# Row sums through HBM in the last image, position terms by transfer, and one addition fewer in cv1

## The chip, the cores and the metric

The kernel runs on one core of a Trainium2 chip. The metric is the device time of one execution in microseconds, and the time of a kernel is the median of several runs. The kernel before takes 2314.39 us (median of 7 runs, 2313.59 to 2315.1). Its profiled execution took 2314.33 us, and the span that the profile covers is 2312.8 us of these, so 1.5 us lie outside it.

All arithmetic is float32. "An image" below is one of the eight elements of the batch, counted 0 to 7. Engines: PE multiplies matrices, DVE and ACT work on vectors, POOL and SP mostly issue transfers.

## The reference

```python
def bot_attention(x, qkv_w, rw, rh):                    # x: 256 channels, 32 x 32 positions
    qkv = conv2d(x, qkv_w, 0).reshape(b, 3, HEADS, HD, hw)   # 4 heads of 64 channels, hw = 1024
    q, k, v = (qkv[:, 0], qkv[:, 1], qkv[:, 2])
    r = (rw + rh).reshape(1, HEADS, HD, hw)             # position terms, one per channel and position
    logits = jnp.einsum('bhdi,bhdj->bhij', q, k + r) * HD ** (-0.5)
    a = jax.nn.softmax(logits, axis=-1)
    return jnp.einsum('bhij,bhdj->bhdi', a, v).reshape(b, c, h, w)

def _L0_conv_ref(x, ...):                               # x is group-normed, 512 channels
    t = cbs(x, cv1_w, cv1_bn, 0)                        # cbs: convolution, batch norm, silu
    ys = [t[:, :C], t[:, C:]]
    for i in range(N):                                  # N = 2 bottlenecks
        yi = ys[-1]
        z = cbs(yi, m_cv1_w[i], m_cv1_bn[i], 1)         # 3x3
        z = bot_attention(z, m_qkv_w[i], m_rw[i], m_rh[i])
        z = jax.nn.silu(bn_eval(conv2d(z, m_cv2_w[i], 0), m_cv2_bn[i]))
        ys.append(yi + z)
    return cbs(jnp.concatenate(ys, axis=1), cv2_w, cv2_bn, 0)

x = x + _L0_conv_ref(_gn(x), ...)                       # eight images
```

## The kernel before

**Stages.** The loop at L1325 runs over the eight images. Each image goes twice (n = 0 and n = 1) through a 3x3 convolution by Winograd tiles (`conv3x3`, L955, matmuls on L970), a projection to q, k and v (`project_strassen`, L611), the attention (`attention_fast`, L709) and a 1x1 convolution (`m2`, L988). Image 0 projects in its n = 0 stage with the plain `project`. The 1x1 convolution cv1 of the next image is done inside the n = 0 stage of the image before; for images 1 to 6 it is one level of Strassen, seven products in place of eight (`strassen_cv1`, L1123). cv2 follows the n = 1 stage.

**Attention.** Queries and heads form four groups (L717): groups 0 and 1 are the two halves of the queries for the first head pair, groups 2 and 3 the same for the second. A group takes its 1024 keys in four pairs of 128-key blocks (L720). For each pair PE makes logits into two PSUM tiles (L734), ACT takes the exponential into an SBUF tile `pt` (L738, three such tiles), DVE adds it to the running sum `acc` of the group (`add_up`, L747), and PE multiplies `pt` by v into the PSUM tile `av_ps` (`times_v`, L757). PE runs one pair ahead: the logits of pair i stand before the product of pair i-1. When a group's product is complete, ACT copies one half of `av_ps` to `ao` (L775) and DVE adds the other (L776); only then may the next group's product overwrite `av_ps`, of which there is one.

**Row sums.** `acc` holds sums over the key blocks, and the 128 partitions are still to be added. After the first logits of the next group, `sums` (L778) does that with four small matmuls against ones (L786), a copy out of PSUM (L792) and a 4 KB store (L793). `spread` (L826), two pairs later, loads the sums (L823), takes the reciprocal `rc` (L830), stores it and loads it broadcast as `rs` (L834). `scale` (L842) multiplies `ao` by it in the next group but one. The last group is summed by `last_sums` (L796) with matmuls on L804, and `rs` is made from PSUM (L880, L881).

**Position terms.** `add_r` (L647) adds `rw` and `rh` to the keys with two DVE instructions a half. For the second head pair `later` (L703) does it, four DVE instructions of 128x512, after the first two pairs of the attention (L856).

**cv1.** `begin` runs at the end of the n = 0 attention: DVE makes eight sums `t_x` (L1159 to L1162), PE makes the products a11 b11 and s4 b22. `go_on` adds a12 b21 onto the first product in PSUM. After `m2`, `rest` makes s1 t1, s2 t2, s3 t3 and a22 t4, each copied out of PSUM by ACT (L1150). `add_y0` and `add_y1` combine them with six DVE additions of 128x1024 in groups 1 and 2 of the n = 1 attention.

**Order.** PSUM has three tiles of two banks under the name "big" for everything but `av_ps`; a new one waits until all readers of the tile in its place are done. Each engine runs its instructions in the order in which the build left them; `issue_after` puts an instruction behind another one of its engine, and the dictionary `behind` names the pair of the attention after which a function's instructions are put in. SP issues most transfers, POOL issues the output stores and residual loads; each issues in order.

Of the kernel before, what the change touches and what calls it, by code (L numbers as in the profile page):

```python
# [41 lines left out]
F32 = mybir.dt.float32  # L45
I32 = mybir.dt.int32
AF = mybir.ActivationFunctionType
ALU = mybir.AluOpType
# [4 lines left out]
P = 128  # L53
# [8 lines left out]
def kernel(  # L62
# [170 lines left out]
    def make_sq(n, tag, bufs):  # L233
        (a11, a12), (a21, a22) = ([block_qkv(n, o, i) for i in range(2)] for o in range(2))
        parts = [act.tile([P, 2, 3, P], F32, tag=tag, name="sq_new", bufs=bufs) for _ in range(2)]
        s1, s2, s3, s4 = (t[:, j] for t in parts for j in range(2))
        nc.vector.tensor_tensor(s1, a21, a22, ALU.add)
        nc.vector.tensor_tensor(s2, s1, a11, ALU.subtract)
        nc.vector.tensor_tensor(s3, a11, a21, ALU.subtract)
        nc.vector.tensor_tensor(s4, a12, s2, ALU.subtract)  # L240
        for h, t in enumerate(parts):
            nc.gpsimd.dma_start(sq_dram[n][:, 2 * h : 2 * h + 2], t)

    def load_sq(n):
        w = ring([P, 4, 3, P], "sq")
# [118 lines left out]
    def stages(act, small, ps_big, ps_av, n_pt):  # L364
# [246 lines left out]
        def project_strassen(n, z, sq, t):  # L611

# [88 lines left out]
                tt(q1, q1, u[:, 0], ALU.add)  # L701

            def later():  # L703
                for half in range(NH):
                    add_r(1, half)

            return q, kr, vT, later

        def attention_fast(n, z, at, behind, sq=None, t=None):  # L709

            q, kr, vT, later = (*project(n, z), None) if sq is None else project_strassen(n, z, sq, t)
            behind.get(-1, lambda: None)()

            ao = act.tile([P, NM, HW], F32, tag="z", name="ao")
# [6 lines left out]
            def logits(pair):  # L723
                g, j0 = pair[0]
                c, half = groups[g]
                pt = act.tile([P, PAIR, 2, HALF], F32, tag="pt", name="pt", bufs=n_pt)
                pts[pair[0]] = pt
                for i, (_, j) in enumerate(pair):
                    ps = ps_big.tile([P, 2, HALF], F32, tag="big", name="l_ps")
                    for hd in range(2):  # L730
                        r = slice(hd * HD, (hd + 1) * HD)
                        for kh in range(2):
                            o = j * P + kh * HD
                            nc.tensor.matmul(  # L734
                                ps[kh * HD : (kh + 1) * HD, hd, :], kr[r, c, o : o + HD],
                                q[r, c, ts(half, HALF)], start=True, stop=True,
                            )
                    exp = nc.scalar.activation(pt[:, i], ps, AF.Exp, scale=SCALE)  # L738
# [39 lines left out]
            def sums(g):  # L778
# [42 lines left out]
            def total(g, s_dram):  # L821

                nc.sync.dma_start(sums_all[:, at + g, :], s_dram.rearrange("a (i r) -> (a i) r", r=QP))  # L823
                return sums_all[:, at + g, :]

            def spread(g, s_dram):  # L826
# [3 lines left out]
                nc.vector.reciprocal(rc, total(g, s_dram))  # L830
# [12 lines left out]

            NQ = NJ // PAIR
            s_drams, rss, evicted = {}, {}, [None]
            for i in range(len(pairs) + 1):
                if i < len(pairs):  # L850
                    added = logits(pairs[i])
                    g, at_q = divmod(i, NQ)
                    with tc.issue_after(added.ins):
                        if at_q == NQ - 2 and g > 0:
                            rss[g - 1] = spread(g - 1, s_drams[g - 1])
                        if i == 1 and later is not None:  # L856
                            later()
                        if at_q == 1 and g > 1:
                            scale(g - 2, rss.pop(g - 2))
                if i > 0:  # L860
                    g, j0 = pairs[i - 1][0]
                    if j0 == 0 and g > 0:
                        s_drams[g - 1] = sums(g - 1)
                    times_v(pairs[i - 1])
                    if i < len(pairs) and accs.get(pairs[i][0][0], 0) is None:
                        with tc.issue_after(evicted[0].ins):
                            added = add_up(pairs[i])
                    with tc.issue_after(added.ins):
                        behind.get(g if j0 == 0 else (g, j0 // PAIR), lambda: None)()
# [253 lines left out]
        def strassen_cv1(w, sw, xts, y0, y1):  # L1123
# [31 lines left out]
            def begin():  # L1155
                t = [act.tile([P, 2, NM, HALF], F32, tag=tag, name="t_x") for tag in ("q", "k")]
                kept["t"] = t1, t2, t3, t4 = [t[i][:, j] for i in range(2) for j in range(2)]
                for c in range(2):
                    tt(t1[:, c], b12[c], b11[c], ALU.subtract)  # L1159
                    tt(t2[:, c], b22[c], t1[:, c], ALU.subtract)  # L1160
                    tt(t3[:, c], b22[c], b12[c], ALU.subtract)
                    tt(t4[:, c], t2[:, c], b21[c], ALU.subtract)  # L1162
                kept["ps"] = product(a11, b11)
                kept["m1"] = to(spare("xr", 2), kept["ps"])
                to(y0_2, product(s4, b22))

            def go_on():
                ps = product(a12, b21, kept["ps"])
# [1 line left out]
                    silu(y0[:, oc, ts(0, HALF)], ps[:, oc, :], bn_cv1 + oc)  # L1170

            def rest():
                t1, t2, t3, t4 = ([t[:, c] for c in range(2)] for t in kept["t"])
# [21 lines left out]
            return begin, go_on, rest, add_y0, add_y1, finish  # L1195

        def cv2_part(w2, ys, oc, ks=range(2 * NM)):

# [126 lines left out]
    for b in range(B):  # L1325
# [89 lines left out]
        ao, check = s.attention_fast(0, z, b * N * NM * NH, behind, sq.get(0), t)  # L1415
# [43 lines left out]

        def first():  # L1460
            if six:
                six[5]()
            if more:
                three[0]()
            else:
# [16 lines left out]
        ao, check = s.attention_fast(1, z, (b * N + 1) * NM * NH, behind, sq.get(1), t)  # L1482
# [105 lines left out]
```

## Time and profile before

| what | value |
|---|---|
| median of 7 runs | 2314.39 us (2313.59 to 2315.1) |
| profiled execution | 2314.33 us |
| its span | 2312.8 us |
| DVE busy | 1839.7 us (80%), 2920 instructions |
| ACT busy | 987.7 us (43%), 1292 instructions |
| POOL busy | 89.1 us (4%), 308 instructions |
| DMA moved | 235.60 MB, mean 102 GB/s |
| one image in the middle (622 to 905 us) | 283.00 us |

The table of engines gives the time that each was busy. PE counts two hardware matmuls for each float32 matmul of the kernel, so "x8" in a row of the trace is four matmuls of the source. The row "one image" is the repeat distance: four of the later images take the same 283 us to within the reading. The chain of waits follows the work that ended last back through the engines. A timeline gives each instruction or run of equal instructions with its start, its duration, and in brackets how long its engine was idle before it. A row for PEld is the loading of a matmul's weights.

### The profile page before, as it was taken

The page shows a single profiled execution, that of the slowest core. Times are in us where ns is not written, and L with a number is a line of the kernel's source. Part 1 is how long each engine was busy: PE and PEld are TensorE (multiplying, and loading weights), DVE is VectorE, ACT ScalarE, POOL GpSimd, SP SyncE. Part 2 cuts the span into 40 slices and gives each one's busy share as a digit, 9 for nine tenths or more (in the row PEclk, how much of TensorE's full clock was granted, in tenths as well). Part 3 has the DMA queues.
Part 4 walks back from the last instruction along what each step waited for, and adds up shares of the span by engine and source line. Part 5 has one row for each costly group of instructions (what it writes and reads, how often), then busy time and mean ns, then how long its engine had stood idle before and what let it go on. Part 6 is the DMA issues. An engine that isn't in the chain of part 4 may idle for free.

```text
span 2312.8 us, 36527 instructions
## 1 busy us (share of the span) xinstructions
PE 2287.2 (99%) x14806; PEld 1172.5 (51%) x14806; DVE 1839.7 (80%) x2920; ACT 987.7 (43%) x1292; POOL 89.1 (4%) x308
## 2 busy tenths in 40 slices
PE   7999999999999999999999999999999999999998
PEld 4546355463554636446364553646436364473633
DVE  8888878888788877887788887788877988777774
ACT  2443524435154452544525354253542535335352
POOL 1000000000000000000000000000000000000000
PEclk9999999999999999999999999999999999999999
DMA  7422334041430415213161221603116030260201
GB/s 239 174 86 87 120 127 161 16 151 34 168 124 21 140 44 201 82 50 111 52 238 38 77 87 47 250 29 102 60 47 250 29 133 29 76 221 16 87 11 62
DMA packets 95521, 235.60 MB, mean 102 GB/s; under 512 B 28016, under 2 KB 50736, under 8 KB 81904
## 3 DMA queue, kind: packets, MB, share of 16 engines
q1 hardware_dynamic: 83600, 182.84, 23.5%
q0 software_dynamic: 11744, 50.34, 5.7%
q8 instruction: 119, 1.95, 0.3%
q14 instruction: 58, 0.48, 0.1%
HBM read 198.54 MB, written 34.60 MB: 101 GB/s over the span
## 4 chain that ended last, share of the span: by engine, by line
PE 96%; DVE 3%; ACT 0%; DMA 0%; POOL 0%; issue 0%; SPq 0%; DVEq 0%; ACTq 0%
PE av_ps L768 19%; PE l_ps L734 19%; PE c_ps L970 14%; PE c L1028 8%; PE p_ps L630 8%; PE x_ps L1140 6%; PE c_new L1028 6%; PE m_ps L994 5%; PE ps L386 4%; PE pv_ps L634 3%; PE s_ps L786 1%; PE p_ps L634 1%; PE s_ps L804 1%; DVE acc L754 0%; PE v_ps L595 0%; DMA x<-in_x_dram 0%
## 5 line engine op out<-in xcount | busy, mean ns | idle before, releaser
L738 ACT ACTIVATE pt<-l_ps 128x1024 f32<-128x1024 f32 x512 | 494.9, 1023 | 410.0 <-PE l_ps L734 385.5
L754 DVE TENSOR_TENSOR acc<-acc,pt 128x1024 f32<-128x1024 f32 x384 | 469.3, 1222 | 65.6 <-ACT pt L738 40.1
L768 PE MATMUL av_ps<-pt,vT 64*64 64x512 f32 x4096 | 486.4, 591 | 0.5 <-DVE ao L776 0.5
L734 PE MATMUL l_ps<-q,kr 64*64 64x512 f32 x4096 | 485.9, 590 | 0.0
L970 PEld LDWEIGHTS c_ps<-v_in,u 128*128 128x128 f32 x2720 | 306.0, 192 | 6.7 <-issue 6.7
L970 PE MATMUL c_ps<-v_in,u 128*128 128x128 f32 x2720 | 306.1, 275 | 0.0
L768 PEld LDWEIGHTS av_ps<-pt,vT 64*64 64x64 f32 x4096 | 159.1, 133 | 269.4 <-issue 223.5
L734 PEld LDWEIGHTS l_ps<-q,kr 64*64 64x64 f32 x4096 | 160.0, 133 | 263.3 <-issue 252.2
L452 ACT COPY m<-c_ps 128x256 f32<-128x256 f32 x96 | 35.4, 369 | 216.8 <-PE c_ps L970 214.1
L1028 PE MATMUL c_new<-t_in,ws 128*128 128x512 f32 x288 | 124.6, 592 | 0.0
L994 PE MATMUL m_ps<-ao,m_sb 128*128 128x512 f32 x256 | 112.5, 592 | 0.0
L369 ACT ACTIVATE m_kept<-m_kept,bh,sh 128x512 f32<-128x512 f32 x42 | 31.9, 806 | 146.0 <-DVE m_kept L1112 86.3
L752 DVE TENSOR_TENSOR acc<-pt 128x1024 f32<-128x1024 f32 x64 | 78.0, 1219 | 18.0 <-ACT pt L738 18.0
L1028 PEld LDWEIGHTS c_new<-t_in,ws 128*128 128x128 f32 x288 | 54.7, 190 | 68.9 <-issue 66.0
L630 PE MATMUL p_ps<-t_z,sq 128*128 128x512 f32 x180 | 87.1, 593 | 0.0
L369 ACT ACTIVATE t<-m_ps,bh,sh 128x512 f32<-128x512 f32 x64 | 48.0, 776 | 83.9 <-PE m_ps L994 82.5
L994 PEld LDWEIGHTS m_ps<-ao,m_sb 128*128 128x128 f32 x256 | 48.6, 190 | 61.2 <-issue 61.0
L369 ACT ACTIVATE z<-z,bh,sh 128x512 f32<-128x512 f32 x64 | 48.6, 806 | 56.0 <-DVE z L481 56.0
L1002 DVE TENSOR_TENSOR ylast<-t,ypad 128x512 f32<-128x512 f32 x32 | 22.0, 692 | 63.3 <-ACT t L369 63.3
L445 DVE TENSOR_TENSOR v_in<-w_rows 128x512 f32<-128x512 f32 x96 | 65.5, 683 | 0.0
L453 DVE TENSOR_TENSOR r_mid<-c_ps,m 128x256 f32<-128x256 f32 x64 | 27.1, 423 | 47.0 <-ACT m L452 47.0
L1028 PE MATMUL c<-ypad,ws 128*128 128x512 f32 x144 | 63.8, 592 | 0.0
(255 smaller groups left out, 2997.1 us busy)
## 6 DMA issues: line engine op xcount, KB each, us to landing
u<-u SPq DMA_DIRECT2D x85, 1024.0 KB
x<-in_x_dram SPq DMA_DIRECT2D x32, 512.0 KB
x_res<-in_x_dram POOLq DMA_DIRECT2D x32, 512.0 KB, 7.0
out_dram<-m_kept POOLq DMA_DIRECT2D x28, 512.0 KB, 7.5
u<-u_new POOLq DMA_DIRECT2D x12, 1024.0 KB, 6.8
w<-in_cv_w_dram SPq DMA_DIRECT2D x12, 1024.0 KB
rs<-r_dram SPq DMA_DIRECT2D x96, 128.0 KB
ws<-s SPq DMA_DIRECT2D x24, 512.0 KB
```

Source lines behind the costliest of these rows:

```text
L369: return nc.scalar.activation(dst, src, AF.Silu, scale=sh[:, k : k + 1], bias=bh[:, k : k + 1])
L386: last_product[0] = nc.tensor.matmul(ps[:, half, :], w_of(k), rhs_of(k, half), start=(k == begin), stop=(k == end))
L630: nc.tensor.matmul(ps[:, o, :], w[:, o, :], rhs, start=not onto, stop=True, skip_group_check=onto)
L634: nc.tensor.matmul(v[:, ts(j, P)], rhs[:, ts(j, P)], w[:, 2, :], start=j == 0 and not onto, stop=True, skip_group_check=True,)
L734: nc.tensor.matmul(ps[kh * HD : (kh + 1) * HD, hd, :], kr[r, c, o : o + HD], q[r, c, ts(half, HALF)], start=True, stop=True,)
L738: exp = nc.scalar.activation(pt[:, i], ps, AF.Exp, scale=SCALE)
L754: ins = nc.vector.tensor_tensor(accs[g], accs[g], pt[:, i], ALU.add)
L768: nc.tensor.matmul(avs[g][hd * HD : (hd + 1) * HD, kh, :], vT[r, j, o : o + HD], pt[r, i, hd, :], start=(j == 0), stop=(j == NJ - 1),)
L970: nc.tensor.matmul(ps[:, row, col, :], us[i][:, k, row, SLOT[col], :], vs[i][:, k, row, col, :], start=(k == 0), stop=(k == NM - 1),)
L994: nc.tensor.matmul(pss[oc][:, half, :], m2_sb[:, n, k, ts(oc, P)], ao[:, k, ts(half, HALF)], start=(k == 0), stop=(k == NM - 1),)
L1028: nc.tensor.matmul(ps[:, o, :], w[:, k, ts(o, P)], rhs[part][:, c, :], start=(k == 0 and not onto), stop=(k == KB - 1), skip_group_check=onto,
L1140: nc.tensor.matmul(ps[:, o, :], w[:, c, ts(o, P)], rhs[c], start=(c == 0 and not onto), stop=(c == 1), skip_group_check=onto,)
```

## The change

1. **Last image only** (`folded`): `sums` with its four matmuls is replaced by `fold`, for groups 0 to 2 of both attentions of image 7. Four stores put the 32-partition quarters of `acc` (128 KB each) into HBM, one load brings back half of it (256 KB), and a POOL transfer adds the other half onto it in SBUF. `total` then adds two halves, transposes 32x32 blocks and reduces on DVE. In these two attentions the first sum of a group's first pair is also put behind the addition of L776, for every group after the first.
2. **Images 2 to 7**: the four DVE additions of `later` are replaced by one POOL transfer of 512 KB that adds the stored sum `rw + rh` onto the keys of the second head pair. The two stored sums are made once, by `make_r`, in the last group of image 1's n = 0 attention: one DVE instruction of 128x1024 and one 512 KB store for each n. The SBUF tiles for it have the tag "xr".
3. **cv1 of images 1 to 6**: s1 t1 is made in `begin` and kept in PSUM until `rest` adds s4 b22 onto it. The sign of t4 is turned, and a22 t4 is added in PSUM onto s3 t3, after ACT has copied s3 t3 out. One DVE addition falls away, and one moves from the second to the third group of the n = 1 attention.

```diff
+    def make_r(n):
+        r = act.tile([P, F, F], F32, tag="xr", name="r_new", bufs=2)
+        nc.vector.tensor_tensor(
+            r, rw_sb[:, n, 1, :].unsqueeze(1).to_broadcast([P, F, F]),
+            rh_sb[:, n, 1, :].unsqueeze(2).to_broadcast([P, F, F]), ALU.add,
+        )
+        nc.gpsimd.dma_start(r_dram[n], r.rearrange("p a b -> p (a b)"))
...
             def later():
-                for half in range(NH):
-                    add_r(1, half)
+                if r_dram is None:
+                    for half in range(NH):
+                        add_r(1, half)
+            if r_dram is not None:
+                nc.gpsimd.dma_start(kr[:, 1, :], r_dram, accum_op=ALU.add)
...
-                if j0 == 0 and g == 1 and later is not None:
+                if j0 == 0 and (g > 0 if folded else g == 1 and later is not None):
                     accs[g] = None
...
+            def fold(g):
+                acc = accs.pop(g).rearrange("p h (a q) -> p (h a) q", a=2)
+                NQ4 = HALF // 2
+                f_dram = tc.dram_tile([2, 2, 4, 32, NQ4], F32, name=f"f_dram{at + g}")
+                for s in range(4):
+                    nc.sync.dma_start(f_dram[s % 2, s // 2].rearrange("a k q -> k a q"), acc[s * 32 : (s + 1) * 32])
+                parts = act.tile([P, 2, NQ4], F32, tag="h", name="fold", bufs=2)
+                nc.sync.dma_start(parts, f_dram[0].rearrange("s a k q -> (a k) s q"))
+                nc.gpsimd.dma_start(parts, f_dram[1].rearrange("s a k q -> (a k) s q"), accum_op=ALU.add)
+                return parts
...
+            def total(g, parts):
+                if not folded:
...
+                a, b = parts[:, 0], parts[:, 1]
+                nc.vector.tensor_tensor(a, a, b, ALU.add)
+                flipped = b.rearrange("p (r k) -> p r k", k=32)
+                nc.vector.transpose(flipped, a.rearrange("p (i r) -> p r i", r=QP))
+                nc.vector.tensor_reduce(sums_all[:, at + g, :], flipped, AX.X, ALU.add)
...
-                        s_drams[g - 1] = sums(g - 1)
+                        folds[g - 1] = fold(g - 1) if folded else sums(g - 1)
...
-                    tt(t4[:, c], t2[:, c], b21[c], ALU.subtract)
+                    tt(t4[:, c], b21[c], t2[:, c], ALU.subtract)
                 kept["ps"] = product(a11, b11)
                 kept["m1"] = to(spare("xr", 2), kept["ps"])
-                to(y0_2, product(s4, b22))
+                kept["ps5"] = product(s1, [t1[:, c] for c in range(2)])
+                kept["m5"] = to(spare("xr", 2), kept["ps5"])
...
-                kept["m5"] = to(spare("xr", 2), product(s1, t1))
+                to(y0_2, product(s4, b22, kept["ps5"]))
                 kept["m6"] = to(spare("x", NX), product(s2, t2))
-                to(y1_2, product(s3, t3))
-                to(y1_1, product(a22, t4))
+                ps = product(s3, t3)
+                to(y1_2, ps)
+                to(y1_1, product(a22, t4, ps))

             def add_y0():
                 tt(kept["m1"], kept["m6"], kept["m1"], ALU.add)
                 tt(y0_2, y0_2, kept["m1"], ALU.add)
-                tt(y0_2, y0_2, kept["m5"], ALU.add)

             def add_y1():
                 tt(y1_2, y1_2, kept["m1"], ALU.add)
-                tt(y1_1, y1_2, y1_1, ALU.subtract)
+                tt(y1_1, y1_1, kept["m1"], ALU.add)
+
+            def add_m5():
                 tt(y1_2, y1_2, kept["m5"], ALU.add)
...
+        if b == 1:
+            behind |= {(NG - 1, n + 1): lambda n=n: make_r(n) for n in range(N)}
+        ao, check = s.attention_fast(0, z, b * N * NM * NH, behind, sq.get(0), t, r_dram[0] if b > 1 else None, not more)
...
-            behind |= {(1, 1): six[3], (2, 1): six[4]}
+            behind |= {(1, 1): six[3], (2, 1): six[4], (3, 1): six[5]}
+        ao, check = s.attention_fast(1, z, (b * N + 1) * NM * NH, behind, sq.get(1), t, r_dram[1] if b > 1 else None, not more)
```

More of the change, by code (lines that the diff above doesn't have):

```diff
@@ L242, in make_sq @@
             nc.gpsimd.dma_start(sq_dram[n][:, 2 * h : 2 * h + 2], t)
+    r_dram = [tc.dram_tile([P, HW], F32, name=f"r{n}") for n in range(N)]
+    def make_r(n):
[5 more added lines that the diff above has]
+        nc.gpsimd.dma_start(r_dram[n], r.rearrange("p a b -> p (a b)"))
     def load_sq(n):
@@ L609, in first_sum, with project_strassen @@
             return t
-        def project_strassen(n, z, sq, t):
+        def project_strassen(n, z, sq, t, r_dram=None):
             q = act.tile([P, NM, HW], F32, tag="q", name="q")
@@ L703, in later, with attention_fast @@
             def later():
-                for half in range(NH):
-                    add_r(1, half)
+                if r_dram is None:
[3 more added lines that the diff above has]
+                nc.gpsimd.dma_start(kr[:, 1, :], r_dram, accum_op=ALU.add)
             return q, kr, vT, later
-        def attention_fast(n, z, at, behind, sq=None, t=None):
-            q, kr, vT, later = (*project(n, z), None) if sq is None else project_strassen(n, z, sq, t)
+        def attention_fast(n, z, at, behind, sq=None, t=None, r_dram=None, folded=False):
+            q, kr, vT, later = (*project(n, z), None) if sq is None else project_strassen(n, z, sq, t, r_dram)
             behind.get(-1, lambda: None)()
@@ L819, in last_total, with spread @@
                 nc.vector.tensor_tensor(sums_all[:, at + g, :], cs[:, 0], cs[:, 1], ALU.add)
-            def total(g, s_dram):
-                nc.sync.dma_start(sums_all[:, at + g, :], s_dram.rearrange("a (i r) -> (a i) r", r=QP))
+            def total(g, parts):
+                if not folded:
+                    nc.sync.dma_start(sums_all[:, at + g, :], parts.rearrange("a (i r) -> (a i) r", r=QP))
+                    return sums_all[:, at + g, :]
+                a, b = parts[:, 0], parts[:, 1]
[3 more added lines that the diff above has]
+                nc.vector.tensor_reduce(sums_all[:, at + g, :], flipped, AX.X, ALU.add)
                 return sums_all[:, at + g, :]
-            def spread(g, s_dram):
+            def spread(g, parts):
                 rs = act.tile([P, HALF], F32, tag="rs", name="rs", bufs=2)
                 rc = small.tile([P, QP], F32, tag="rc", name="rc", bufs=2)
-                nc.vector.reciprocal(rc, total(g, s_dram))
+                nc.vector.reciprocal(rc, total(g, parts))
                 r_dram = tc.dram_tile([2, HALF], F32, name=f"r_dram{at + g}")
@@ L847, in attention_fast @@
             NQ = NJ // PAIR
-            s_drams, rss, evicted = {}, {}, [None]
+            folds, rss, evicted = {}, {}, [None]
             for i in range(len(pairs) + 1):
@@ L854, in attention_fast @@
                         if at_q == NQ - 2 and g > 0:
-                            rss[g - 1] = spread(g - 1, s_drams[g - 1])
+                            rss[g - 1] = spread(g - 1, folds.pop(g - 1))
                         if i == 1 and later is not None:
@@ L1172, in rest @@
             def rest():
-                t1, t2, t3, t4 = ([t[:, c] for c in range(2)] for t in kept["t"])
-                kept["m5"] = to(spare("xr", 2), product(s1, t1))
+                _, t2, t3, t4 = ([t[:, c] for c in range(2)] for t in kept["t"])
+                to(y0_2, product(s4, b22, kept["ps5"]))
                 kept["m6"] = to(spare("x", NX), product(s2, t2))
-                to(y1_2, product(s3, t3))
-                to(y1_1, product(a22, t4))
+                ps = product(s3, t3)
+                to(y1_2, ps)
+                to(y1_1, product(a22, t4, ps))
             def add_y0():
@@ L1193, in finish @@
                             silu(dst[:, oc, :], dst[:, oc, :], bn + oc)
-            return begin, go_on, rest, add_y0, add_y1, finish
+            return begin, go_on, rest, add_y0, add_y1, add_m5, finish
         def cv2_part(w2, ys, oc, ks=range(2 * NM)):
@@ L1414 @@
             behind[-1] = lambda: make(1, 0, range(PAIRS))
-        ao, check = s.attention_fast(0, z, b * N * NM * NH, behind, sq.get(0), t)
+        if b == 1:
+            behind |= {(NG - 1, n + 1): lambda n=n: make_r(n) for n in range(N)}
+        ao, check = s.attention_fast(0, z, b * N * NM * NH, behind, sq.get(0), t, r_dram[0] if b > 1 else None, not more)
         made = None
@@ L1461, in first @@
             if six:
-                six[5]()
+                six[6]()
             if more:
@@ L1480 @@
         if six:
-            behind |= {(1, 1): six[3], (2, 1): six[4]}
-        ao, check = s.attention_fast(1, z, (b * N + 1) * NM * NH, behind, sq.get(1), t)
+            behind |= {(1, 1): six[3], (2, 1): six[4], (3, 1): six[5]}
+        ao, check = s.attention_fast(1, z, (b * N + 1) * NM * NH, behind, sq.get(1), t, r_dram[1] if b > 1 else None, not more)
         ylast = act.tile([P, NM, HW], F32, tag="v", name="ylast")
```

## The prediction

> **What bounds the kernel now.** First the table of engines on the page; then one image out of the middle, as a window (columns: length, then busy time and instructions of PE, PEld, DVE, ACT and POOL, then granted clock, DMA share, GB/s).
>
> ```profile
> PE 2287.2 (99%) x14806; PEld 1172.5 (51%) x14806; DVE 1839.7 (80%) x2920; ACT 987.7 (43%) x1292; POOL 89.1 (4%) x308
> 622.00:905.00 283.00, 283.00 (x1850) 145.45 (x1849) 227.86 (x353) 123.26 (x160) 8.95 (x33) 1.00 0.29 100
> ```
>
> PE is busy for 283.00 of 283.00 us at a granted clock of 1.00; a window over 300 to 2270 us gives 1970.00 of 1970.00. Thus time changes only where PE gets fewer matmuls or begins to wait. DVE has 55 us to spare in each image. The change takes from DVE twelve times four additions of 0.65 us (31 us) and six of 1.22 us in cv1 (7 us): nothing of that is on PE's path, and I cost it at nothing. The cover is PE's own work.
>
> **Removed: six sets of row-sum matmuls.** The chain of waits, in image 7's n = 0 attention (start, length):
>
> ```profile
> 2093.10 1.72 PE l_ps L734 x16
> 2094.82 0.57 PE s_ps L786 x8
> 2095.39 1.88 PE av_ps L768 x16
> 2097.26 1.72 PE l_ps L734 x16
> ```
>
> A set takes 0.57, and the product behind it 1.88 where others take 1.72: 0.73 us. Three groups in two attentions make 6 sets: **-4.4**. In images 1 to 6 the sets stay. The product now comes 0.73 earlier after the eviction L776. Elsewhere (image 1) that addition ends 1.38 us after the preceding product, and PE's first matmul, with one logits set of 1.72 between, wants it by about 1.5. I take no stall; at 0.2 in each of six places it would be +1.2.
>
> **Moved: s1 t1 into `begin`.** PE's amount of work stays; what it waits for changes. In time order, image 1's cv1, and last a pair of rows from the tail of the kernel:
>
> ```profile
> 440.09 0.69 DVE L1159 TENSOR_TENSOR t_x<-x 128x512 f32<-128x512 f32 x1
> 440.22 3.60 PE L1140 MATMUL x_ps<-x,sw 128*128 128x512 f32 x8
> 448.31 7.03 PE L994 MATMUL m_ps<-ao,m_sb 128*128 128x512 f32 x16
> 448.51 1.45 ACT L369 ACTIVATE y<-x_ps,bh,sh 128x512 f32<-128x512 f32 x2 [2.53 <-PE x_ps L1140]
> 465.47 3.60 PE L1140 MATMUL x_ps<-t_x,w 128*128 128x512 f32 x8
> 465.67 1.01 ACT L1150 COPY ypad<-x_ps 128x1024 f32<-128x1024 f32 x1 [2.42 <-PE x_ps L1140]
> ...
> 2284.33 0.30 PEld L386 LDWEIGHTS ps<-ypad,w 128*128 128x128 f32 x2 [0.55 <-ACT t L369]
> 2284.44 1.02 PE L386 MATMUL ps<-ypad,w 128*128 128x512 f32 x2
> ```
>
> - *t1 in time?* The second product starts at 440.22 and takes 0.43 a matmul; its third, the first with t1's second half, is due at 441.08. That half is ready at 440.09 + 0.69 = 440.78. In images 2 to 6 the same margin, 0.3 us, remains: no stall. If it were gone: as much as DVE is late, six times.
> - *Image 1* has `make_r`'s two 128x1024 additions before that point on DVE, 1.22 each as in L752's rows: 2.43. t1 is ready at 443.21; about 0.16 for the restart (weights loaded 0.11 before the matmul in the pair above, 0.05 for the signal); minus 441.08: **+2.3**. Queued behind on DVE are t2 to t4, wanted after `m2`. The two stores of 512 KB stand on POOL; the copies of the two products take over their tiles and wait for them to land: 3.3 us by the row of sw_new, 7.0 by that of x_res below. In the second case the sums of `last_sums`, copied behind them on ACT, and so `m2`'s first tile come some 1.2 us late: +2.1 to +3.5.
> - *m2's second tile.* It now takes the PSUM place that `go_on`'s first two silu free, at 448.51 + 1.45 = 449.96; PE wants it after four source matmuls, 448.31 + 4 x 0.43 = 450.02. With 0.16 for the restart 0.1 remains; in six images **+0.6** (0 to 0.3 each: 0 to 1.8).
> - *a22 t4 onto s3 t3.* It must wait for the copy of s3 t3: 465.67 + 1.01 = 466.68. Up to then PE has five Winograd matmuls (the built order of instructions puts them in between), 0.2235 each (192 passes in 21.44, two a matmul): 465.47 + 1.12 = 466.59. So 0.09 + 0.16 = 0.25 in each of six images: **+1.5** (0.05 to 0.45 each, as the restart is cheap or dear: 0.3 to 2.7).
>
> The Trainium skill, "Perfetto Trace Analysis", Optimizing Tensor Performance / Matmuls, says that independent matmul groups should rotate through PSUM banks so that evacuating one overlaps the next one's matmuls. That speaks against this edit: without the five matmuls in between the wait would be 1.37 x 6 = 8.2. The copy's row and the order shrink it to 1.5; no run yet shows which holds.
>
> **Put in place of the sums: the fold.** The chain of transfers has to be shorter than its cover. DVE in image 7 after the first group, and the transfers that come nearest (KB, us to landing):
>
> ```profile
> 2099.25 2.56 DVE L754 TENSOR_TENSOR acc<-acc,pt 128x1024 f32<-128x1024 f32 x2 [0.58 <-ACT pt L738]
> 2101.72 0.20 DVE L830 RECIPROCAL rc<-sums_all 128x8 f32<-128x8 f32 x1
> 2108.25 0.69 DVE L776 TENSOR_TENSOR ao<-av_ps,ao 128x512 f32<-128x512 f32 x1
> ```
>
> ```profile
> out_dram<-t POOLq DMA_DIRECT2D x6, 256.0 KB, 2.3
> x_res<-in_x_dram POOLq DMA_DIRECT2D x32, 512.0 KB, 7.0
> sw<-sw_new POOLq DMA_DIRECT2D x2, 512.0 KB, 3.3
> ```
>
> Group 0's last exponential ends at about 2089.1; with `later` gone from DVE its sum is complete 2.5 later, at 2091.6. DVE comes to `fold`'s arithmetic (behind the row at 2099.25) at 2101.1 if nothing waits. Behind it stand the reciprocal, one pair's additions (2.47) and, last, L776, which frees `av_ps` for PE. L776 should end 1.5 us after the group's product, 2106.66 + 1.5 = 2108.16. Backwards: 0.69 + 2.47 + 0.20 + three small operations (0.42 for 128x256 by L453's row, so 1.27; 0.20 to 0.69 each by the reciprocal's and L776's rows) = 4.63; the data may come as late as 2103.5. **Cover: 11.9 us** (11.1 to 12.6 by the bounds of the three).
>
> The chain: four stores issued in 0.35 to 0.52 each, landing 2.3 after the last issue: 3.7 to 4.4. The load: 0.5 + 2.3 = 2.8. The adding transfer: no row shows one. 256 KB without adding took 2.3, 512 KB up to 7.0; with up to 0.7 to issue, 3.0 to 7.1. In all 9.5 to 14.3. I take 4.2 for the last, nearer to the row of its size, and about 11 in all: **0** on PE's path, the cover being DVE's other additions. Longer than 11.9, every us counts in four places (groups 0 and 1 of two attentions; behind the third no product follows that waits), up to 2.4 x 4 = +9.6. SP issues three transfers more a fold than with `sums` and its load, about 1.5 us; behind them stand r_dram's store and the broadcast loads, wanted a group later.
>
> The Trainium skill, "Collectives: The Full Stack", Part 3 on the bandwidth ceiling, says that an adding transfer reads two sources and runs at half the rate (it measured 1.93). By that 256 KB would go like 512, 3.3 to 7.0: the chain were 10.5 to 14.3, the middle of it past the cover.
>
> **Keys by transfer, images 2 to 7.** It waits for the last DVE instruction that writes those keys, at about 2077.7 in image 7, and the second head pair's logits start at 2103.95: 26 us of cover against 7.0 for 512 KB. One-sided cost 0; the quiet DMA of an attention covers it. Doubled to 14 it is still hidden, and a gain is excluded as DVE is not waited for. Behind it on POOL stand the memsets of the next `w_rows` and, some 50 us later, the next loads; POOL is 4% busy.
>
> **Sum**: -4.4 + 2.3 + 0.6 + 1.5 + 0 = 0.0. The profiled execution took 2314.33 (span 2312.8 and 1.5 around it), the median is 2314.39: forecast **2314.4**. With the low ends, -4.4 + 2.1 + 0 + 0.3 = -2.0: 2312.4. With the high ends but the fold covered, -4.4 + 1.2 + 3.5 + 1.8 + 2.7 = +4.8: 2319.2.
>
> **Rivals.**
> A, *the fold arrives late*: DVE sits at the first fold operation, L776 behind it is late, and PE waits before the next group's product, in four places. It decides from a chain of 11.9 us; at 14 it costs 2.1 x 4 = 8.4, with the rest 2322.8, slower. For it: three transfers one after the other, one of an unseen kind. Against: the rows at their short ends sum to 9.5.
> B, *all restarts hidden*: the signals are quick and the margins of 0.1 to 0.3 us suffice; then only -4.4 and, where DVE slips make_r in earlier than I think, little of the 2.3: 2310 to 2312. For it: the margins are that small.
> C, *the keys are late*: a 512 KB adding transfer over 26 us, 12 times. At 28: +24, 2338. Against: nothing seen takes over 7.5.
> D, *relief of DVE pays*: PE's matmuls run faster with less DVE traffic or a wait that the profile doesn't show ends; below 2309.8. Against it 1970.00 of 1970.00.
>
> **How the numbers follow.** This kernel's runs lie within 1.5 us; 0.2% (4.6 us) is what a measurement can be asked to tell from no change, so "same" is 2309.8 to 2319.0. Forecast as summed 0.58; A 0.19, of which 0.17 beyond 2319.0 (below that a chain of 12 to 13 us); B 0.14, nearly all within; C 0.03; D 0.06. Faster 0.06, slower 0.20 + 0.02 from the high ends = 0.22, same 0.72. The range takes B and the shorter half of A: 2310.5 to 2321.5; the forecast's own is 2312.4 to 2319.2.
>
> **What would show it.** The chain in image 7 without s_ps rows, product and logits next to each other; PE idle of 2.3 us before the third matmul of image 1's second x_ps product, released by DVE t_x; some 0.25 before the last x_ps matmuls, released by ACT's copy, in six images; no idle time of PE before av_ps in image 7. An idle PE there, with DVE idle before its 128x256 addition, is A; before l_ps of the third group, C. The forecast is wrong if one image of 283 us changes by over 0.7.

## The result and the profile after

The changed kernel takes 2320.26 us (median of 14 runs, 2318.23 to 2321.84) against 2314.43 for the kernel before (34 runs, 2312.46 to 2315.27): ratio 1.0026, 95% interval 1.0019 to 1.0033. It is 5.8 us slower. The time lies inside the range, but on the side of rival A: the forecast was "no change", and its own range ended at 2319.2. The profiled execution took 2319.68 us, its span is 2318.2.

From the page of the changed kernel, the table of engines and the chain that ended last, by engine:

```profile
PE 2287.4 (99%) x14758; PEld 1172.1 (51%) x14758; DVE 1816.7 (78%) x2886; ACT 985.9 (43%) x1286; POOL 108.1 (5%) x328
PE 92%; DVE 4%; DMA 2%; issue 1%; ACT 0%; POOL 0%; SPq 0%; DVEq 0%; POOLq 0%; ACTq 0%
```

PE has 48 hardware matmuls fewer and is no less busy; 2% of the chain is now transfers. The view of PE's waits (what it waited for: us in total, times, longest) has two lines that are new and one that has grown from 0.5:

```profile
PE av_ps L784 <- DVE ao L792: 4.5, 3, 2.4
PE x_ps L1177 <- DVE t_x L1196: 1.5, 2, 0.8
PE ps L399 <- DVE ao L792: 0.5, 1, 0.5
```

Waits and busy time don't give the whole difference, since a PE that goes slowly counts as busy. So the two traces are compared at fixed points: how much later than in the trace of before does the same matmul start? The first matmul of each m2 serves. Such a difference also holds where the execution began; before image 1 that differs by -1.2 to +1.0 us from trace to trace, and only the steps are read.

| from one m2 to the next | predicted | measured step |
|---|---|---|
| image 1, up to m2 of n = 0 | +2.3 | +1.98 |
| then each of images 1 to 6, once | 0.25 + 0.1 | +0.33 to +0.35 |
| sum over images 1 to 6 | +4.4 | +4.05 |
| image 7, n = 0 attention | -2.2 | +2.21 |
| image 7, n = 1 attention and up to m2 | -2.2 | +0.36 |

The steps sum to 6.6, the spans differ by 5.4; the rest is the start (-0.6) and what lies behind the last matmul (8.8 us here, 9.4 before).

**cv1.** Three rows of the timeline of the changed kernel, two of image 1 and one of image 2 (start, length, and in brackets the idle time before):

```profile
440.52 1.12 PE L1177 MATMUL x_ps<-t_x,sw 128*128 128x512 f32 x2 [0.78 <-DVE t_x L1196]
442.32 2.84 PE L1177 MATMUL x_ps<-t_x,sw 128*128 128x512 f32 x6 [0.68 <-DVE t_x L1196]
...
751.57 2.84 PE L1177 MATMUL x_ps<-t_x,w 128*128 128x512 f32 x6
```

In image 1 PE waits for both halves of t1, 1.5 us in the brackets and 2.0 by the table. In image 2 the a22 t4 product starts at 751.57, where the five Winograd matmuls in front of it began at 750.30 and last 5 x 0.2235 = 1.12: 0.15 later than they end, with no bracket.

**The fold.** The chain of waits in the n = 0 attention of image 7 (start, length, what; the pieces of "issue" and of queues left out):

```profile
2099.01 2.78 DMA fold<-f_dram
...
2102.53 4.43 DMA fold<-f_dram
...
2106.99 0.43 DVE fold L857
...
2111.12 0.69 DVE ao L792
...
2112.47 2.51 DMA f_dram<-acc
...
2115.11 2.80 DMA fold<-f_dram
...
2118.63 4.64 DMA fold<-f_dram
...
2123.30 0.44 DVE fold L857
...
2127.43 0.69 DVE ao L792
...
2128.17 2.38 PE av_ps L784 x16
2130.55 2.98 PE l_ps L750 x16
```

Read it from above. Group 0's sum is complete at 2095.49; the last of its three transfers lands at 2106.96, 11.5 us later. DVE folds, and only then makes the last two additions into the sum of group 1 and the eviction, which ends at 2111.80; PE's product of group 2 starts 0.06 late. Group 1's sum is therefore complete at 2111.2, 15.7 us after group 0's, where a group of PE takes 13.7. Its transfers take another 12.1 us, and its fold ends so late that the eviction ends at 2128.11 and the product of group 3 starts at 2128.17, 2.5 us after the logits before it are done (2123.92 + 1.72 by the timeline). The folds hang on one another.

The last two lines show something else: 2.38 and 2.98 us for pieces that take 1.72. Windows of the changed kernel over that place (length, PE, PEld, DVE, ACT, POOL, then the granted clock, DMA share, GB/s):

```profile
2124.00:2128.00 4.00, 1.82 (x20) 0.38 (x12) 3.83 (x6) 2.52 (x3) 0.00 (x0) 1.00 0.04 7
2128.00:2130.00 2.00, 1.83 (x16) 0.72 (x20) 1.90 (x3) 0.00 (x0) 0.00 (x0) 0.89 0.83 227
2130.00:2132.00 2.00, 2.00 (x12) 0.52 (x8) 1.90 (x3) 0.00 (x0) 0.00 (x0) 0.50 0.51 154
2132.00:2134.00 2.00, 2.00 (x20) 0.77 (x16) 1.15 (x2) 1.43 (x2) 0.00 (x0) 0.76 0.47 131
```

After the stall PE's granted clock falls to 0.50 and comes back within some 4 us. The next product starts at 2133.35 by the timeline: 5.18 us for two pieces of 1.72, so 1.74 us lost besides the stall. In the n = 1 attention PE was idle for 1.71 us and the clock stayed at 1.00.

### The profile page after: what moved, and what is told of

Same layout as the page of the kernel before. It is cut to its first block, busy times and chain, and to the rows that moved or that the text cites. A ratio compares the mean times of both kernels' runs of the same rounds, so it can differ in the third digit from the quotient of the medians.

```text
span 2318.2 us, 36502 instructions
## 1 busy us (share of the span) xinstructions
PE 2287.4 (99%) x14758; PEld 1172.1 (51%) x14758; DVE 1816.7 (78%) x2886; ACT 985.9 (43%) x1286; POOL 108.1 (5%) x328
## 3 DMA queue, kind: packets, MB, share of 16 engines
q8 instruction: 118, 1.93, 0.3%
## 4 chain that ended last, share of the span: by engine, by line
PE 92%; DVE 4%; DMA 2%; issue 1%; ACT 0%; POOL 0%; SPq 0%; DVEq 0%; POOLq 0%; ACTq 0%
PE av_ps L784 17%; PE l_ps L750 17%; PE c_ps L1006 14%; PE c L1064 8%; PE p_ps L643 8%; PE c_new L1064 6%; PE x_ps L1177 6%; PE m_ps L1030 5%; PE ps L399 4%; PE pv_ps L647 3%; DMA fold<-f_dram 2%; PE p_ps L647 1%; PE s_ps L802 1%; DVE acc L770 1%; PE s_ps L833 1%
## 5 line engine op out<-in xcount | busy, mean ns | idle before, releaser
L1177 PE MATMUL x_ps<-t_x,sw 128*128 128x512 f32 x144 | 64.1, 594 | 1.5 <-DVE t_x L1196 1.5
```

The costliest lines, as they stand in the source:

```text
L1177: nc.tensor.matmul(ps[:, o, :], w[:, c, ts(o, P)], rhs[c], start=(c == 0 and not onto), stop=(c == 1), skip_group_check=onto,)
```

## The experiments

The theory after the result is called "loop" below: a round of fold, last additions, transfers, next fold takes longer than a group of PE, and the lack is handed on. Its rival, "single", is the prediction's rival A as it was put: each fold for itself is late beyond 11.9 us. Twelve kernels were run, each with 4 to 11 timed runs beside the kernel before (medians of that 2313.79 to 2313.94).

### The first part alone

```diff
-        ao, check = s.attention_fast(0, z, ..., r_dram[0] if b > 1 else None, not more)
+        ao, check = s.attention_fast(0, z, ..., None, not more)
```
(the same for n = 1, without `make_r`, and cv1 as before)

> The kernel before with the first part of the change alone (row sums through HBM in the last image). Theory 'loop': fold g is read by DVE ahead of the last additions into the sum of group g+1, so fold g+1 cannot start before fold g has landed; a round is 11.5 (transfers) + 1.6 + 0.2 + 2.5 = 15.8 us against the 13.7 us of a group of PE, and the lack is handed on. Without the second part DVE also has its four additions of 0.65 us in the first group, so fold 0 starts 2.6 us later and is itself late: a stall before the product of group 2 of about 2.6 us and one before that of group 3 of about 2.2, in both attentions: -4.4 + 9.6 = +5, with the slow PE clock after a stall up to +7.5: 2319.5 to 2322. Rival 'single': each fold is late by itself only where its own chain exceeds 11.9 us, the stalls are those of the changed kernel, +2 to +3: 2316.5 to 2317.5.

Measured 2323.84 us (2320.36 to 2326.92), ratio 1.0048 (1.0034 to 1.0061): +10. PE's timeline in the n = 0 attention of image 7, the two products that waited:

```profile
2110.88 1.95 PE L784 MATMUL av_ps<-pt,vT 64*64 64x512 f32 x16 [1.32 <-DVE ao L792]
...
2127.08 3.28 PE L784 MATMUL av_ps<-pt,vT 64*64 64x512 f32 x16 [2.23 <-DVE ao L792]
```

Two stalls an attention now, since `later` with its four additions is back on DVE and the first fold starts some 2.2 us later (its sum is complete at 2094.94 here, where the trace lies 0.65 behind that of the kernel before, and at 2095.49 in the changed kernel's, which lies 3.42 behind). In the n = 1 attention PE waits 1.12 and 1.91 us in the same places, and 0.48 before the product of group 1. The second product takes 3.28 in place of 1.95: the slow clock again, and again 1.74 us (the next product starts at 2132.26). The step of this attention is +3.88, the next one's +3.72, from the table's points. "Loop" holds: the two steps sum to 7.6, at the upper end of what was expected. The median, +10, lies above that; the rest wasn't followed. The run also shows what the second part of the change is good for: it lets the first fold start in time.

### The third part alone, and the second alone

The third part (cv1 as after; everything else as before):

> The kernel before with the third part alone (cv1). Theory: 0.10 us a time for the second tile of m2 and 0.25 for the wait on ACT's copy, six images: +2.1, 2316.5, and no PE wait for t_x in image 1. Rival: these offsets between the two traces come from something else (the transfers into the keys, DVE's load): then 2314.4.

Measured 2316.28 us (2315.31 to 2316.86), ratio 1.0012 (1.0003 to 1.0021): +2.5. The steps are +0.33 to +0.35 in each of six images, +2.06 in all, and no wait for t_x is left in PE's list.

The second part (position terms by transfer; everything else as before):

> The kernel before with the second part alone (position terms by transfer). Theory: no PE wait gained or lost: 2314.4, between 2313.5 and 2315.3, with DVE's busy time about 31 us lower. Rival 'relief pays': under 2312.

Measured 2313.94 us (2313.78 to 2316.51), ratio 1.0004 (0.9995 to 1.0013). DVE is busy 1815.4 us, 24 less where 31 was expected, and from image 1 on every step between the m2 points is 0.01 or less. A relief of DVE that PE doesn't wait for buys nothing by itself. The adding transfer of 512 KB lands in 5.5 us (5.3 to 6.8) in the changed kernel; the cover was 26.

### Only the middle fold

```diff
-                        folds[g - 1] = fold(g - 1) if folded else sums(g - 1)
+                        folds[g - 1] = fold(g - 1) if folded and g == 2 else sums(g - 1)
```

> The changed kernel, but in the last image only group 1 goes through HBM; groups 0 and 2 are summed by matmuls again (four sets of 0.73 us back). 'Loop': nothing delays the sum of group 1, its transfers of about 11.5 us start on time and PE has no wait over 0.3 us before the product of group 3, no slow clock there: against the changed kernel +2.9 (matmuls) - 4.4 - 1.9 - 0.6 (stalls gone) = -4.0, about 2316.3. 'Single': the fold of group 1 is late on its own account, the two stalls of 2.4 and 1.7 us before group 3 stay: +2.9 - 0.6 = about 2322.5.

Measured 2318.29 us (2317.37 to 2319.02), ratio 1.0021 (1.0012 to 1.0030). The median is 2 us above the expectation, the stage is as expected: PE has no wait there, and the steps of image 7 are -0.73 and -0.72, one set of matmuls each. DVE's timeline (n = 0 attention):

```profile
2120.45 0.42 DVE L857 TENSOR_TENSOR fold<-fold 128x256 f32<-128x256 f32 x1 [0.57 <-DMA fold<-f_dram]
...
2126.07 0.69 DVE L792 TENSOR_TENSOR ao<-av_ps,ao 128x512 f32<-128x512 f32 x1 [1.40 <-ACT ao L791]
```

The same fold that stalls PE by 2.4 us in the changed kernel makes DVE wait 0.57 us here, and the eviction waits for ACT, not for it. What differs is that no fold went before it, and that the matmul sets of groups 0 and 2 are back. The set of group 2, 0.73 us, stands before the product that waited and is too short to hide 2.4. "Single" falls. What lifts the median above the steps wasn't followed; in the profiled execution 0.65 us of it lies behind the last matmul.

### Reading the folds one group later

```diff
+                        if at_q == 1 and g > 1 and folded:
+                            rss[g - 2] = spread(g - 2, folds.pop(g - 2))
-                        if at_q == NQ - 2 and g > 0:
+                        if at_q == NQ - 2 and g > 0 and not folded:
...
-                        if at_q == 1 and g > 1:
+                        if at_q == (NQ - 1 if folded else 1) and g > 1:
                             scale(g - 2, rss.pop(g - 2))
...
+            if folded:
+                with tc.issue_after(evicted[0].ins):
+                    rss[g - 1] = spread(g - 1, folds.pop(g - 1))
             ps, rows, s_dram = last_sums(g)
```

> The changed kernel with the folded sums read by DVE one group later (behind the first two pairs of the next group but one; the last one behind the last eviction), so that nothing of the next sum stands behind a transfer. 'Loop': no PE wait before the products of groups 2 and 3, no slow clock; from the first projection product of image 7 on, the first attention gets 4.4 us shorter than in the changed kernel and the second 1.9: about 2313.9, plus what the third fold, now ready only after the last product, costs at m2 (0 to 3 in each attention). Rival 'clock or contention': PE is slow in these places because of the transfers themselves, at least 2 of the 4.4 us stay.

Measured 2313.09 us (2312.37 to 2313.91): ratio to the kernel before 0.9996 (0.9987 to 1.0005), 7 us under the changed kernel. The window over the same stage:

```profile
2100.00:2140.00 40.00, 40.00 (x346) 14.47 (x339) 30.37 (x35) 22.64 (x25) 3.76 (x5) 1.00 0.36 80
```

PE 40.00 of 40.00 at a clock of 1.00, with the same transfers running. The steps of image 7 are -2.19 and -2.18: exactly three sets of 0.73 each. The slow clock came from the stall, not from the transfers, and the third fold costs nothing at m2 here.

### Two plain loads in place of the adding transfer

```diff
-                nc.gpsimd.dma_start(parts, f_dram[1].rearrange("s a k q -> (a k) s q"), accum_op=ALU.add)
+                nc.gpsimd.dma_start(other, f_dram[1].rearrange("s a k q -> (a k) s q"))
...
+                nc.vector.tensor_tensor(parts, parts, others.pop(g), ALU.add)
                 a, b = parts[:, 0], parts[:, 1]
```

> The changed kernel with the adding transfer replaced by a plain load of the second half into a tile of its own and one more DVE addition of 128x512. 'Loop': the chain falls from 11.5 to about 7.5 us, a round to 7.5 + 2.3 + 0.2 + 2.5 = 12.5 us, under the 13.7 of a group: no stall, 2313.5 to 2314. Rival 'queue': what makes the folds late is SP's queue (the broadcast loads in front of the stores), 1 to 2 us of stalls stay in each attention: 2316 or more.

Measured 2313.29 us (2311.88 to 2314.27), ratio 0.9997 (0.9988 to 1.0006); steps of image 7 -2.19 and -2.18 again. From the views by tile, first the adding transfer of the changed kernel (ns to issue, min, median, max) and its landing:

```profile
L822 POOL DMA_DIRECT2D fold<-f_dram x6: 1179/1192/1207, 2102.5 to 2265.4; - x6
...
DMA to landing us min/median/max: 4.3/4.5/4.8
```

and the plain one of this kernel:

```profile
L825 POOL DMA_DIRECT2D other<-f_dram x6: 707/720/735, 2100.2 to 2255.5; - x6
...
DMA to landing us min/median/max: 2.9/3.1/3.4
```

The adding transfer of 256 KB lands in 4.5 us where the plain one takes 3.1, takes 1.19 us to issue in place of 0.72, and must wait for the load that it adds onto, which the plain one need not. DVE pays 0.68 us a fold for that and doesn't wait for a fold at all. "Queue" falls as what makes PE wait: SP still issues the two broadcast loads (1.10 us) straight before the stores of the second fold, and there is no stall. The Trainium skill, "Collectives: The Full Stack", Part 3 on the bandwidth ceiling, puts the ReduceScatter of a ring, whose steps add, at half the rate of an AllGather, a ratio of 1.93, and says that its model holds for rings alone; the ratio of the landings of these single transfers is 4.5 / 3.1 = 1.45.

### make_r in an earlier group

```diff
-            behind |= {(NG - 1, n + 1): lambda n=n: make_r(n) for n in range(N)}
+            behind |= {(NG - 3, n + 1): lambda n=n: make_r(n) for n in range(N)}
```

> The changed kernel with the two additions and stores of make_r put into the second group of image 1's attention in place of the last. Theory: the 2.05 us between the traces in image 1 go, nothing else changes: 2318.2, no PE wait for t_x. Rival: the delay comes from the moved product itself (its PSUM tile, its copy), it stays: 2320.3.

Measured 2316.34 us (2314.55 to 2318.14), ratio 1.0011 (1.0002 to 1.0020). The wait for t_x is gone from PE's list, and the step up to m2 in image 1 falls from +1.98 to +0.59. The 0.59 is make_r's in its new place: the combined kernel below, without the cv1 part, has +0.61 there and in PE's list a second wait of 0.5 us for an eviction. Yet the kernel is more than expected below the changed one, because in image 7 the transfers were a little quicker (the first two chains 11.0 and 11.4 us): the stalls are 1.33 and 1.26 us, the clock stays at 1.00, and the steps are -0.63 and -0.18 instead of +2.21 and +0.36. Why the transfers were quicker is not known. A stall that stays short escapes the second price.

### a22 t4 in a PSUM tile of its own

```diff
-                ps = product(s3, t3)
-                to(y1_2, ps)
-                to(y1_1, product(a22, t4, ps))
+                to(y1_2, product(s3, t3))
+                to(y1_1, product(a22, t4))
...
-                tt(y1_1, y1_1, kept["m1"], ALU.add)
+                tt(y1_1, y1_2, y1_1, ALU.add)
```

> The changed kernel with a22 t4 in a PSUM tile of its own again (and the addition of t4's product to y1_2 in its old form), s1 t1 still in `begin`. Theory: of the 0.34 us an image that images 2 to 6 lose, the 0.25 of the wait for ACT's copy go and the 0.10 at m2's second tile stay; 6 x 0.25 = 1.5 us less than the changed kernel, 2318.8 or a little under. Rival: the loss belongs to the product moved into `begin`, the 0.34 stay.

Measured 2319.18 us (2317.47 to 2323.08), ratio 1.0025 (1.0016 to 1.0034). The steps of images 1 to 6 fall from 0.34 to 0.08 to 0.10 each: the 0.25 belonged to the wait for ACT's copy, the 0.10 stays. In the timeline of image 2 the products stand end to end, with no Winograd matmuls between them:

```profile
743.06 7.03 PE L1177 MATMUL x_ps<-t_x,sw 128*128 128x512 f32 x16
749.93 3.60 PE L1177 MATMUL x_ps<-t_x,w 128*128 128x512 f32 x8
```

The median is 5.3 us above the kernel before beside it, the changed kernel's was 5.8: the 1.5 of the steps can't be read off it. The stalls of image 7 vary from one execution to the next. Nothing was changed there, and yet the steps are -0.20 and +2.14 in this trace (PE idle for 1.76 and 2.40 us, the slow clock behind the second alone), against +2.21 and +0.36 in that of the changed kernel.

### Without the cv1 part, and how far it carries

Groups 0 and 1 only, read one group later, everything else as before:

> The kernel before with only groups 0 and 1 of the last image through HBM, read one group later as above; group 2 stays with matmuls; no other part of the change. 'Loop': 4 sets of 0.73 us fall away and no wait appears, although DVE still has its four additions in the first group: -2.9, 2311.5. If DVE's load there mattered as in the run with the fold alone: 2314 or more.

Measured 2311.76 us (2310.62 to 2312.55), ratio 0.9990 (0.9981 to 0.9999). The steps of image 7 are -1.12 and -1.10, not -1.46: the first product of group 1 starts 0.3 late, behind the eviction. On DVE the eviction stands without a gap behind the last additions into the sum (2089.57 to 2094.78), and these behind the four additions of `later`: in the run that reads the folds later on the changed kernel, without these additions, the same product starts on time. The cover that the prediction took for granted there does run out, by 0.3 us, where those additions stay.

With the second part (make_r early), all three folds read later:

> The kernel before with the first part, its sums read one group later, and the second part with make_r in the second group of image 1; no change of cv1. 'Loop': six sets of matmuls fall away, each attention of image 7 is 2.2 us shorter and PE gets no new wait: 2314.0 - 4.4 = 2309.6. Against the run with two folds it also shows the 0.3 us that DVE's additions in the first group cost there gone.

Measured 2309.95 us (2309.05 to 2311.21), ratio 0.9983 (0.9974 to 0.9992), steps -2.19 and -2.18, and no 0.3 us at group 1: it is 4.0 us below the kernel before that ran beside it, and some 10 below the changed one.

The same in more images:

> As last_combined, but the row sums go through HBM in all images but the first: 14 attentions with three sets each. If DVE and the transfers keep up: 14 x 2.2 = 30.7 us less, 2283. Against it: in the n = 1 attention of images 1 to 6 DVE also has five or six additions of 1.22 us for cv1 in groups 1 and 2, and a group would need 11.3 + 1.7 + 3.7 = 16.7 of its 13.7 us on DVE; then PE waits up to 3 us in each of two groups, twelve attentions halved: 2290 to 2310.

> As last_combined, with the sums through HBM in the n = 0 attention of images 1 to 7 and in both of the last image: 8 attentions, 8 x 2.2 = 17.6 us less, 2296.4, if the transfers of the next image (u, w, sq) on the same queue don't hold the stores up; if they do, PE waits before the products, up to no gain at all: 2314.

Measured 2347.96 us (ratio 1.0146, 1.0131 to 1.0162) and 2351.93 (1.0166, 1.0152 to 1.0180). Both expectations missed, and most of the loss has none of the reasons that were named. All images, image 2, first DVE and then PE:

```profile
737.80 0.20 DVE L867 RECIPROCAL rc<-sums_all 128x8 f32<-128x8 f32 x1
742.93 0.69 DVE L879 TENSOR_TENSOR ao<-ao,rs 128x512 f32<-128x512 f32 x1 [4.93 <-DMA rs<-r_dram]
```

```profile
743.68 8.74 PE L1035 MATMUL m_ps<-ao,m_sb 128*128 128x512 f32 x14 [4.38 <-DVE ao L879]
```

In the n = 0 attention of images 1 to 6 the last eviction stands behind eight sums of cv1 on DVE, and the third fold behind it; its scale then waits 4.9 us for the broadcast loads and m2 4.4 us for the scale, with the clock at 0.50 behind it. Six such waits are 28.4 us, before the slow clock. The view of PE's waits has two lines more that the combined kernel has not, or has with 1.0 us only:

```profile
PE av_ps L784 <- DVE ao L792: 9.7, 8, 2.4
PE l_ps L750 <- DVE gm L518: 7.4, 6, 1.8
```

Of the first, six waits of 1.2 to 2.4 us stand before products of the n = 1 attentions, where a stall had been expected; the second are logits that take over the PSUM tile with the means of the group norm. DVE copies these out (L518) behind a scale, and the scale waits for its broadcast loads, 0.67 us in image 2. With the folds in the n = 0 attentions alone the first line stays at 0.8, and PE waits 30.7 us before m2 and 8.6 before logits: the transfers of the next image, which had been named there, weren't in the way of the products. Leaving the third set to matmuls in these images, as in the run with two folds, was not tried; whether the gain of the last image can be had in the others stays open.

## Why the prediction was right and wrong

- *Removed sets, -4.4.* Right: three sets give -2.19 and -2.18 wherever nothing waits.
- *Image 1, +2.3.* Right in size and cause: 1.98, in two waits, one for each half of t1, where one of 2.3 was put before the second half; and PE's wait is gone when make_r stands earlier, where it costs 0.6 at another place.
- *m2's second tile, +0.1 each, and a22 t4, +0.25 each.* Right, to 0.02 us: 0.33 to 0.35 together, 0.08 to 0.10 without the second. The rule on rotating PSUM banks that was weighed there spoke against this edit with reason; the five matmuls kept it to 0.25.
- *Keys by transfer, 0.* Right.
- *The fold, 0.* Wrong; this step failed. The chain was well sized: 11.5 measured against "about 11", with 3.5 for the stores, 2.8 for the load and 5.2 for the adding transfer with its issue (4.2 was taken; the upper bound of 7.1 should have been 7.0 + 0.7 = 7.7, which nothing here came near). The cover of 11.9 us was right too, for group 0: its product was late by 0.06. The error lies in "Cover: 11.9 us" being applied to each fold. Group 1's sum is complete only when DVE has done the additions that stand behind fold 0, so it starts its chain late. In a round stand the chain, the three operations, the reciprocal and the last additions: 11.5 + 1.6 + 0.2 + 2.5 = 15.8 us, against a group of 13.7. The point from which it decides is not 11.9 but 13.7 - 4.3 = 9.4 us. Two plain loads come under it, the chain as built does not.
- *Rival A* had the mechanism and the sign, not the places: of its four, the two of group 0 did not wait, and "behind the third no product follows that waits" was off by the 0.5 us that the tail waited in the n = 1 attention. Nor had it the second price, the clock: 1.7 us for one of two stalls.

In sum the image-7 terms measured +2.6 where -4.4 was predicted, and the others 4.05 for 4.4. That the time still lies in the range isn't the merit of the sum: the range had been stretched from 2319.2 to 2321.5 for rival A. And where in it the time fell was in part luck, since the stalls of image 7 differ between executions: its two steps together are +2.6 in the trace of the changed kernel, +1.9 with a22 t4 in its own tile and -0.8 with make_r early, with the same folds.

## What to carry to other kernels

When a result comes back by a slow way and is read in order on a busy engine, don't compare its latency with the slack of one pass only: write down the round, from this reading to the work that feeds the next sending, and compare that with the period. If it is longer, reading one period later mends it without making anything faster. On an engine that works in order, put an instruction that waits for a slow transfer behind the work that another engine waits for. And a PE stall of about two microseconds can cost its own length and 1.7 us more in slow clock.

## What the hardware showed that was not expected

The granted clock fell to 0.50 after PE had been idle for 1.91, 2.23, 2.35 and 2.40 us in these traces, and stayed at 1.00 after 1.12, 1.26, 1.32, 1.33, 1.71 and 1.76 us (in each case before a product of image 7, released by the eviction). Behind each of these four falls the two following pieces together took 1.74 to 1.75 us longer, which is what some 3.5 us at half the clock lose. The Trainium skill, "TensorE: Matmul & The Clock Gate", Part 1, says that the clock falls after at least one idle window of about 3.4 us and rises after a busy one. The way up agrees with the 3.5 us; for the fall less sufficed here.

The traces also show where such a window begins. In each of the fourteen, all changes of the granted clock lie whole multiples of 3.41 us apart, wherever the stalls are. Let these steps of 3.41 us be laid over the whole trace, and PE's idle time be counted within each step. Between 300 and 2295 us, each of the 17 steps at full clock in which PE was idle for 1.91 us or more has 0.50 in the next one; after each of the 27 with 1.07 to 1.90 us it stays at 1.00. So the length of a stall alone doesn't decide. This one, of the kernel with the folds in the n = 0 attentions, is longer than two of the four stalls with a fall, and the clock stays at 1.00:

```profile
1293.19 1.95 PE L750 MATMUL l_ps<-q,kr 64*64 64x512 f32 x16 [2.31 <-DVE gm L518]
```

A step ends at 1292.67 and parts it into 1.79 and 0.52. Why some 1.9 us of idle time in a step are enough, and whether other matmuls around it move that figure, no run shows.

A StreamTranspose of 128x256 took 0.64 us where an addition of that size took 0.42.
